# The first layer's mixtures and state layer, from three stages to one written order

## The chip, the cores and the metric

The kernel runs on one core of one Trainium2 chip, as one launch. The metric is the device time of that launch in microseconds, the median of several runs. A core has TensorE (PE, its weight loads PEld), VectorE (DVE), ScalarE (ACT), GpSimd (POOL), and SyncE (SP), whose queue issues most DMAs. Each engine works through a queue of its own and waits on semaphores for the other engines' results.

## What is computed

The input x has 4 sequences of 1024 tokens with 128 channels, all in 32-bit floats. Two layers follow; only the first one is touched here:

```
x = x + 0.5 * moe0(layernorm(x))
x = x + s6(layernorm(x))
x = x + 0.5 * moe0(layernorm(x))          # the same weights again
# the second layer: a capped mixture, attention over 16 wavelengths, the mixture again

moe0(h): probs = softmax(h @ w_router.T); w = the best two of 8, divided by their sum
         sum over those two of w_e * (relu(h @ w1_e.T)**2 @ w2_e.T)
         + relu(h @ ws1.T)**2 @ ws2.T     # shared, 256 hidden channels

s6(h):   u, res = split(h @ W_in)                      # 256 channels each
         u = silu(causal convolution of u over 3 tokens)
         dt, B, C = split(u @ W_x)                     # 8, 16, 16
         delta = softplus(dt @ W_dt + b_dt); A = -exp(A_log)
         s_n[t] = exp(delta * A_n) * s_n[t-1] + delta * u * B_n[t]     # n = 0..15
         y = sum over n of s_n * C_n + u * D
         return (y * silu(res)) @ W_out
```

## The kernel before, in words

x stays in SBUF as `x_sb`, tokens on partitions, 32 tiles of 128 tokens; a group is one sequence, 8 tiles. Three stages, `moe0`, `s6`, `moe0`, run one after another. In each, the tile framework's planner orders the instructions of every engine, from the order in the text, the dependencies and the number of buffers of each tile.

`moe0` computes every expert for every token and weighs with zero where a token did not choose it. For each group: `layernorm_t` (statistics on VectorE, normalized tiles transposed by TensorE, copied out by ScalarE), `route` (router logits, best two by rank counting), then for each half of 512 tokens two shared hidden units and eight experts. `hidden` is a matmul hp (L181), relu on ScalarE (L183), square on GpSimd (L185); hp has three PSUM buffers and h four, so several units are under way at once. The second matmul op (L195, L214) has three PSUM buffers, and VectorE adds each expert's result into x_sb with its weight, one tile of 128 tokens at a time (L218). A matmul of 32-bit floats is two passes on TensorE, so each appears twice in the counts.

`s6` works per sequence with channels on partitions (two halves c of 128). Input matmul pin (L264), convolution by three VectorE instructions (L273, L277), silu u (L285), W_x matmul into xd (L291, L298), then softplus by hand (L308 to L323: sp_v, sp_z, sp_w, delta, du). The recurrence runs in two stretches of 512 tokens. For each state n:

```
bp = sel[:, n].T @ xd        # TensorE spreads row n of B over 128 partitions (L334)
cp = sel[:, NS + n].T @ xd   # and row n of C (L336), copied to c_sb by ScalarE (L338)
for c in 0, 1:
    da = exp(delta * A_n)           # ScalarE (L341)
    db = du * bp                    # VectorE (L345)
    hst = scan(da, db)              # VectorE, the recurrence (L347)
    last = hst[:, 511]              # GpSimd, in the first stretch (L356)
    hm = hst * c_sb                 # GpSimd (L358)
    yp[c] += ident.T @ hm           # TensorE sums over n in PSUM (L359)
```

At its end y is formed (L364, L372), multiplied with W_out (L376) and added to x_sb (L384). The second mixture follows for all groups; then `moe1`, which uses `layernorm_t` and `route` too, the attention, whose TensorE and VectorE orders are written out by hand, and `moe1` again.

Of the kernel before, what the change touches and what calls it, by code (L numbers as in the profile page):

```python
# [20 lines left out]
I32 = mybir.dt.int32  # L21
# [55 lines left out]

def ln_stats(nc, sb, x, mv, rstd):

    n = x.shape[1]  # L80
    for i in range(n):
        st = sb.tile([P, nc.vector.BN_STATS_DIM], F32, name="ln_st", bufs=4)
        nc.vector.bn_stats(st, x[:, i, :])
        nc.vector.bn_aggr(mv[:, i, :], st)

    a = sb.tile([P, n], F32, name="ln_a")
    nc.vector.tensor_scalar(a, mv[:, :, 1], EPS, None, op0=ALU.add)
    q = sb.tile([P, n], F32, name="ln_q")
    nc.vector.tensor_scalar(
        rstd.bitcast(I32), a.bitcast(I32), -0.5, RSQRT, op0=ALU.mult, op1=ALU.add  # L90
    )
    for _ in range(3):
        nc.vector.scalar_tensor_tensor(q, rstd, -0.5, rstd, op0=ALU.mult, op1=ALU.mult)
        nc.vector.tensor_tensor(q, q, a, op=ALU.mult)
        nc.vector.scalar_tensor_tensor(rstd, q, 1.5, rstd, op0=ALU.add, op1=ALU.mult)
# [24 lines left out]
def route(nc, k, sb, ps, xnt, w_router, ex, mask):  # L120


    lg = ps.tile([P, GT, E], F32, name="lg", tag="tr")
    for i in range(GT):
        nc.tensor.matmul(lg[:, i, :], xnt[:, ts(i, P)], w_router, start=True, stop=True)
    mx = sb.tile([P, GT], F32, name="rt_mx")
    nc.vector.tensor_reduce(mx, lg, AX.X, ALU.max)
    d = sb.tile([P, GT, E], F32, name="rt_d")
    nc.vector.tensor_tensor(d, lg, mx[:, :, None].to_broadcast([P, GT, E]), op=ALU.subtract)
    nc.scalar.activation(ex, d, AF.Exp)  # L130
# [5 lines left out]
    eq = sb.tile([P, GT, E, E], F32, name="rt_eq")  # L136
    nc.vector.tensor_tensor(eq, other, own, op=ALU.is_equal)
    nc.vector.tensor_tensor(
        eq, eq, k.tri[:, None, :, :].to_broadcast([P, GT, E, E]), op=ALU.mult
    )  # L140
    above = sb.tile([P, GT, E, E], F32, name="rt_above")
# [6 lines left out]

def moe0(tc, k):


    nc = tc.nc
    with (
        tc.tile_pool(name="m0", bufs=2) as sb,
        tc.tile_pool(name="m0_tr", bufs=2, space=PSUM) as ps_tr,
        tc.tile_pool(name="m0_h", bufs=3, space=PSUM) as ps_h,
        tc.tile_pool(name="m0_o", bufs=3, space=PSUM) as ps_o,  # L160
    ):
        for g in range(B):
            xnt = sb.tile([P, L], F32, name="xnt")
            layernorm_t(nc, k, sb, ps_tr, g, xnt)
            ex = sb.tile([P, GT, E], F32, name="ex")
            mask = sb.tile([P, GT, E], F32, name="mask")
            route(nc, k, sb, ps_tr, xnt, k.wr0, ex, mask)

            w = sb.tile([P, GT, E], F32, name="w")
            nc.vector.tensor_tensor(w, ex, mask, op=ALU.mult)  # L170
            tot = sb.tile([P, GT], F32, name="tot")
            nc.vector.tensor_reduce(tot, w, AX.X, ALU.add)
            nc.vector.reciprocal(tot, tot)
            nc.vector.scalar_tensor_tensor(
                w, w, 0.5, tot[:, :, None].to_broadcast([P, GT, E]), op0=ALU.mult, op1=ALU.mult
            )

            def hidden(w1, cols):

                hp = ps_h.tile([P, 512], F32, name="hp")  # L180
                nc.tensor.matmul(hp, w1, xnt[:, cols], start=True, stop=True)  # L181
                r = sb.tile([P, 512], F32, name="r", bufs=3)
                nc.scalar.activation(r, hp, AF.Relu)  # L183
                h = sb.tile([P, 512], F32, name="h", bufs=4)
                nc.gpsimd.tensor_tensor(h, r, r, op=ALU.mult)  # L185
                return h

            for half in range(2):
                cols = ts(half, 512)
                t0 = g * GT + half * 4  # L190
                hs = [hidden(k.ws1[:, ts(f, P)], cols) for f in range(FS)]
                op = ps_o.tile([P, 4, C], F32, name="op")
                for i in range(4):
                    for f in range(FS):
                        nc.tensor.matmul(  # L195
                            op[:, i, :],
                            hs[f][:, ts(i, P)],
                            k.ws2[:, f, :],
                            start=(f == 0),
                            stop=(f == FS - 1),  # L200
                        )
                nc.vector.scalar_tensor_tensor(
                    k.x_sb[:, t0 : t0 + 4, :],
                    op,
                    0.5,
                    k.x_sb[:, t0 : t0 + 4, :],
                    op0=ALU.mult,
                    op1=ALU.add,
                )
                for e in range(E):  # L210
                    h = hidden(k.w1_0[:, e, :], cols)
                    op = ps_o.tile([P, 4, C], F32, name="op")
                    for i in range(4):
                        nc.tensor.matmul(  # L214
                            op[:, i, :], h[:, ts(i, P)], k.w2_0[:, e, :], start=True, stop=True
                        )
                    for i in range(4):
                        nc.vector.scalar_tensor_tensor(  # L218
                            k.x_sb[:, t0 + i, :],
                            op[:, i, :],  # L220
                            w[:, half * 4 + i, e : e + 1],
                            k.x_sb[:, t0 + i, :],
                            op0=ALU.mult,
                            op1=ALU.add,
                        )
# [5 lines left out]
def s6(tc, k):  # L231

    nc = tc.nc
    HL = 512
    with (
        tc.tile_pool(name="s6_c", bufs=1) as cst,
        tc.tile_pool(name="s6_b", bufs=2) as sb,
        tc.tile_pool(name="s6_w", bufs=3) as wk,
        tc.tile_pool(name="s6_tr", bufs=2, space=PSUM) as ps_tr,
        tc.tile_pool(name="s6_bc", bufs=2, space=PSUM) as ps_bc,  # L240
        tc.tile_pool(name="s6_y", bufs=1, space=PSUM) as ps_y,
    ):

        NR = DTR + 2 * NS
        sel = cst.tile([NR, 2 * NS, P], F32, name="sel")
        nc.vector.tensor_copy(sel, k.ident[0:NR, DTR:NR, None].to_broadcast([NR, 2 * NS, P]))
# [4 lines left out]
        for b in range(B):  # L251
            xnt = sb.tile([P, L], F32, name="xnt", bufs=1)
            layernorm_t(nc, k, sb, ps_tr, b, xnt)


            u = sb.tile([P, DI, L], F32, name="u")
            res = sb.tile([P, DI, L], F32, name="res")
            for c in range(2 * DI):
                if c < DI:
                    up = sb.tile([P, L + 2], F32, name="up", bufs=1)  # L260
                    nc.gpsimd.memset(up[:, 0:2], 0.0)
                for half in range(2):
                    pin = ps_tr.tile([P, HL], F32, name="pin", tag="tr")
                    nc.tensor.matmul(  # L264
                        pin, k.w_in[:, ts(c, P)], xnt[:, ts(half, HL)], start=True, stop=True
                    )
                    if c < DI:
                        nc.scalar.copy(up[:, 2 + half * HL : 2 + (half + 1) * HL], pin)
                    else:
                        nc.scalar.activation(res[:, c - DI, ts(half, HL)], pin, AF.Silu)  # L270
                if c < DI:
                    cv = sb.tile([P, L], F32, name="cv", bufs=1)
                    nc.vector.tensor_scalar(  # L273
                        cv, up[:, 0:L], k.w_conv[:, c, 0:1], None, op0=ALU.mult
                    )
                    for j in (1, 2):
                        nc.vector.scalar_tensor_tensor(  # L277
                            cv,
                            up[:, j : j + L],
                            k.w_conv[:, c, j : j + 1],  # L280
                            cv,
                            op0=ALU.mult,
                            op1=ALU.add,
                        )
                    nc.scalar.activation(u[:, c, :], cv, AF.Silu)  # L285

            xd = sb.tile([NR, L], F32, name="xd")
            for half in range(2):
                pxd = ps_tr.tile([NR, HL], F32, name="pxd", tag="tr")
                for c in range(DI):  # L290
                    nc.tensor.matmul(  # L291
                        pxd,
                        k.w_x[:, c, :],
                        u[:, c, ts(half, HL)],
                        start=(c == 0),
                        stop=(c == DI - 1),
                    )
                nc.scalar.copy(xd[:, ts(half, HL)], pxd)  # L298

# [862 lines left out]
```

## Time and profile before

| | us |
|---|---|
| median of 3 runs | 8650.8 |
| lowest and highest run | 8642.78, 8652.74 |
| the profiled execution's own time | 8645.76 |
| its span on the core | 8644.0 |
| first mixture stage, to about | 195 |
| state layer, about 195 to | 1111 |
| second mixture stage, last add at about | 1291 |

A window's row gives for each engine the time it was busy and the number of instructions, then the granted TensorE clock as a share of full speed. A group's row gives line, engine, operation, the tiles written and read, the count, the busy time in us with the mean ns of one, and the idle time of the engine just before them, with what ended it. In a waits row stand who waited, on whom, the total in us, the times and the longest. A busy TensorE is not TensorE at its peak: the end of a matmul is modelled, and its pipeline's latency is in it.

### The profile page before, as it was taken

The page shows a single profiled execution, that of the slowest core. Times are in us where ns is not written, and L with a number is a line of the kernel's source. Part 1 is how long each engine was busy: PE and PEld are TensorE (multiplying, and loading weights), DVE is VectorE, ACT ScalarE, POOL GpSimd, SP SyncE. Part 2 cuts the span into 40 slices and gives each one's busy share as a digit, 9 for nine tenths or more (in the row PEclk, how much of TensorE's full clock was granted, in tenths as well). Part 3 has the DMA queues.
Part 4 walks back from the last instruction along what each step waited for, and adds up shares of the span by engine and source line. Part 5 has one row for each costly group of instructions (what it writes and reads, how often), then busy time and mean ns, then how long its engine had stood idle before and what let it go on. Part 6 is the DMA issues. An engine that isn't in the chain of part 4 may idle for free. (4 is left out here: it accounts for less than half of the span.)

```text
span 8644.0 us, 174023 instructions
## 1 busy us (share of the span) xinstructions
PE 7278.9 (84%) x76602; PEld 3189.2 (37%) x76602; DVE 6580.4 (76%) x14818; ACT 7447.6 (86%) x1746; POOL 621.7 (7%) x642
## 2 busy tenths in 40 slices
PE   8888886888888888888888988888888888888885
PEld 5222253333333333333333433333334333333333
DVE  6766676777777777777777777777777777777773
ACT  2333324999999999999999999999999999999993
POOL 3554440000000000000000000000000000000000
PEclk9777797999999999999999999999999999999996
DMA  0000000000000000000000000000000000000000
GB/s 19 0 0 0 0 6 4 2 1 2 1 1 2 1 1 2 2 1 1 2 1 1 1 1 1 2 1 2 1 1 1 1 1 1 1 1 2 1 1 16
DMA packets 14660, 20.06 MB, mean 2 GB/s; under 512 B 3242, under 2 KB 12978, under 8 KB 13876
## 3 DMA queue, kind: packets, MB, share of 16 engines
q8 instruction: 611, 10.01, 0.5%
q1 hardware_dynamic: 9572, 6.01, 0.2%
q10 hardware_dynamic: 4304, 2.62, 0.1%
q14 instruction: 173, 1.42, 0.1%
HBM read 6.53 MB, written 2.10 MB: 1 GB/s over the span
## 5 line engine op out<-in xcount | busy, mean ns | idle before, releaser
L870 ACT ACTIVATE p_w<-xs,cc 128x7936 f32<-128x7936 f32 x1024 | 6971.4, 6898 | 92.3 <-PE o L880 73.9
L880 PE MATMUL o<-p_w,vt 128*9 128x256 f32 x63488 | 3829.5, 387 | 700.7 <-ACT p_w L870 695.2
L880 PEld LDWEIGHTS o<-p_w,vt 128*9 128x9 f32 x63488 | 1792.2, 92 | 2590.9 <-ACT p_w L870 1065.2
L789 DVE SCALAR_TENSOR_TENSOR x_p<-x_p,x_r 128x256 f32<-128x256 f32 x3072 | 1306.3, 425 | 105.4
L888 DVE COPY os<-o 128x256 f32<-128x256 f32 x1024 | 431.9, 422 | 580.4 <-PE o L880 579.5
L765 DVE COPY xs<-s 128x1024 f32<-128x1024 f32 x512 | 626.5, 1224 | 203.6 <-PE s L729 202.2
L743 DVE TENSOR_REDUCE nm<-s 128x1 f32<-128x1024 f32 x512 | 625.6, 1222 | 200.0 <-PE s L729 199.7
L880 PE MATMUL o<-p_w,vtop 128*9 128x256 f32 x2048 | 626.0, 388 | 9.8 <-DVE vtop L803 9.8
L906 PE MATMUL pt<-ident,os 128*128 128x128 f32 x2048 | 455.0, 304 | 168.7 <-DVE os L888 162.7
L729 PE MATMUL s<-kp,qp 32*128 32x512 f32 x2048 | 587.0, 650 | 0.7 <-DVE nm L743 0.7
L729 PE MATMUL s<-qp,kp 32*128 32x512 f32 x2048 | 583.1, 646 | 0.0
L906 PEld LDWEIGHTS pt<-ident,os 128*128 128x128 f32 x2048 | 208.2, 142 | 926.5 <-DVE os L888 789.0
L790 DVE SCALAR_TENSOR_TENSOR p_w<-x_p,x_e 128x256 f32<-128x256 f32 x1024 | 435.8, 426 | 109.4 <-DVE x_p L789 3.2
L359 PE MATMUL yp<-hm,ident 128*128 128x512 f32 x512 | 387.7, 878 | 105.5 <-POOL hm L358 103.9
L699 POOL COPY wp_q<-c_wq 128x32 f32<-128x32 f32 x32 | 6.9, 215 | 6151.4 <-PE pq L708 6151.4
L341 ACT ACTIVATE da<-delta,neg_a 128x512 f32<-128x512 f32 x256 | 182.7, 721 | 305.2 <-DVE hst L347 304.7
L787 DVE SCALAR_TENSOR_TENSOR x_p<-x_r 128x256 f32<-128x256 f32 x1024 | 429.1, 419 | 0.1
L781 DVE TENSOR_TENSOR x_r<-x_r,x_p 128x256 f32<-128x256 f32 x1024 | 428.5, 419 | 0.0
L358 POOL TENSOR_TENSOR hm<-hst,c_sb 128x512 f32<-128x512 f32 x256 | 369.9, 1457 | 172.6 <-ACT c_sb L338 119.7
L774 DVE TENSOR_SCALAR x_r<-xs,cc 128x256 f32<-128x256 f32 x1024 | 353.1, 345 | 1.0
L778 DVE TENSOR_SCALAR x_e<-x_p 128x256 int32<-128x256 f32 x1024 | 301.6, 295 | 35.0
L776 DVE TENSOR_SCALAR x_p<-x_r 128x256 f32<-128x256 f32 x1024 | 301.5, 294 | 35.0
(189 smaller groups left out, 4816.6 us busy)
## 6 DMA issues: line engine op xcount, KB each, us to landing
x_sb<-in_L_attn_x_dram ACTq DMA_DIRECT2D x4, 512.0 KB
c_w<-in_L_ffn_w_dram SPq DMA_DIRECT2D x4, 512.0 KB
out_dram<-x_sb SPq DMA_DIRECT2D x4, 512.0 KB
c_w<-in_L_ffn_w_stack_dram SPq DMA_DIRECT2D x1, 512.0 KB
c_w<-in_L_ffn_w_stack_dram ACTq DMA_DIRECT2D x1, 512.0 KB
c_ws<-in_L_ffn_ws_dram SPq DMA_DIRECT2D x2, 128.0 KB
c_w_in<-in_L_attn_W_in_dram SPq DMA_DIRECT2D x1, 256.0 KB
c_w_out<-in_L_attn_W_out_dram SPq DMA_DIRECT2D x1, 128.0 KB
```

Source lines behind the costliest of these rows:

```text
L359: nc.tensor.matmul(yp[c], k.ident, hm, start=(n == 0), stop=(n == NS - 1))
L729: nc.tensor.matmul(s[:, ts(half, 512)], a[row, ts(i, P)], c[row, ts(half, 512)], start=True, stop=True,)
L743: nc.vector.tensor_reduce(nm[:, i, 0:1], score(j, qp[n], i, kp[n]), AX.X, ALU.max, negate=True)
L765: nc.vector.tensor_copy(xs[u][:, i, :], score(j, kp[n], i, qp[n]))
L781: nc.vector.tensor_tensor(r, r, p, op=ALU.subtract)
L787: nc.vector.scalar_tensor_tensor(p, r, EXP2[4], r, op0=ALU.add, op1=ALU.mult)
L789: nc.vector.scalar_tensor_tensor(p, p, c, r, op0=ALU.add, op1=ALU.mult)
L790: nc.vector.scalar_tensor_tensor(p_w[g][:, 0, 0:SOFT], p, EXP2[0], e.bitcast(F32), op0=ALU.add, op1=ALU.mult,)
L870: nc.scalar.activation(p_w[g].rearrange("p a b -> p (a b)")[:, SOFT:], xs[u].rearrange("p a b -> p (a b)")[:, SOFT:], AF.Exp, scale=cc[:, ...
L880: nc.tensor.matmul(o[32 * r : 32 * r + D + 1, 0:QW], vtop[u] if soft else vts[b % 2][:, i, h, :], p_w[g][:, i, ts(r, QW)], start=(i == 0), ...
L888: nc.vector.tensor_copy(os, o[:, 0:QW])
L906: nc.tensor.transpose(pt[:, wl % 2 * 2 + c, :], os[:, ts(c, P)], k.ident)
```

## The change

`moe0` and `s6` become one stage, `layer0`. All five queues follow the order in which its text emits instructions. Its pieces are Python generators that yield after a small step, so that the steps of one can be laid between those of another.

- The mixtures are numbered m = 0 to 7: m < 4 is the first mixture of sequence m, m >= 4 the second of sequence m - 4. `route_rows` normalizes (by ScalarE's Identity with scale and shift), routes, and writes the square roots of the weights as 8 rows into DRAM; `weights` reads four of them back for a half, spread over 128 partitions by DMA. `experts` then scales relu(hp) by that root on GpSimd, squares on ScalarE, and sums all ten units of a half in one PSUM tile, which VectorE adds to x_sb once. hp and op have one PSUM buffer each.
- `prepare` folds the convolution into three accumulating matmuls with scaled copies w_cv of W_in, and writes the rows of B and C to DRAM. `states` takes 1024 tokens at once: rows of B and C arrive by DMA spread over 128 partitions (bc, three buffers, issued two states ahead), VectorE multiplies, scans, and a state later multiplies with C in place; the matmuls into y follow two states behind. `close` forms the output; its alternating partner is `softplus` of the next sequence.
- Beside the states of sequence b run the first mixture of b + 1 and, after it, the second of b - 1 and routing of others: three mixture steps for each of the first ten states, two afterwards. Mixture 0 and the second mixture of sequence 3 stand alone at the start and the end. After the first mixture of b + 1, one step of `prepare` is laid into each state.
- `route` is split (`best_two`, `rsqrt` become functions), with exp issued behind the ranking; `rt_eq` and `rt_above` have one buffer. `moe1` uses it too. w_conv is now loaded as rows spread over 128 partitions.

The core of the diff:

```diff
-def moe0(tc, k):
-def s6(tc, k):
...
+def layer0(tc, k):
+    HL = 512
...
+        tc.tile_pool(name="l0_y", bufs=1, space=PSUM) as ps_y,
+        tc.tile_pool(name="l0_t", bufs=1, space=PSUM) as ps_t,
+        tc.tile_pool(name="l0_r", bufs=1, space=PSUM) as ps_r,
+        tc.tile_pool(name="l0_h", bufs=1, space=PSUM) as ps_h,
+        tc.tile_pool(name="l0_o", bufs=1, space=PSUM) as ps_o,
+        tc.manual_schedule(engines=engines),
+    ):
         neg_a = cst.tile([P, DI, NS], F32, name="neg_a")
         nc.scalar.activation(neg_a, k.a_log, AF.Exp)
         nc.vector.tensor_scalar(neg_a, neg_a, -1.0, None, op0=ALU.mult)
+        w_cv = cst.tile([C, 3, DI * P], F32, name="w_cv")
+        for j in range(3):
+            nc.vector.tensor_tensor(w_cv[:, j, :], k.w_in[:, 0 : DI * P], ...)
...
+        def experts(m, half, after):
+            op = ps_o.tile([P, 4, C], F32, name="op")
+            for i in range(n + 2):                      # n = FS + E
+                if i == 1:
+                    weights(m, half, 1)
+                if i == 7 and after:
+                    weights(*after, 0)
+                if i >= 2:
+                    j = i - 2
...
+                    for a in range(4):
+                        nc.tensor.matmul(op[:, a, :], h[j][:, ts(a, P)], w2,
+                            start=(j == 0 and a == 0), stop=(j == n - 1 and a == 3))
+                if i < n:
...
+                    hp = ps_h.tile([P, HL], F32, name="hp")
+                    nc.tensor.matmul(hp, w1, m_x[m][:, ts(half, HL)], start=True, stop=True)
+                    r[i] = mb.tile([P, HL], F32, name="r", bufs=3)
+                    nc.scalar.activation(r[i], hp, AF.Relu, scale=ROOT if i < FS else 1.0)
+                if 1 <= i <= n:
+                    j = i - 1
+                    if j >= FS:
+                        e = j - FS
+                        nc.gpsimd.tensor_tensor(
+                            r[j], r[j], m_w[m, half, e // 4][:, e % 4, :], op=ALU.mult)
+                    h[j] = mb.tile([P, HL], F32, name="h", bufs=3)
+                    nc.scalar.activation(h[j], r[j], AF.Square)
+                yield
+            nc.vector.tensor_tensor(
+                k.x_sb[:, t0 : t0 + 4, :], k.x_sb[:, t0 : t0 + 4, :], op, op=ALU.add)
...
+        def states(b):
...
+            for s in range(NS + 2):
+                if s + 2 < NS:
+                    rows(s + 2)                         # DMA: B_n and C_n to 128 partitions
+                if s + 1 < NS:
+                    decay(s + 1)                        # ScalarE: two exp of 1024
+                if s < NS:
+                    for c in range(DI):
+                        hs[s, c] = sb.tile([P, L], F32, name="hs", bufs=6)
+                        nc.vector.tensor_tensor(hs[s, c], du[b][:, c, :], bc[s][:, 0, :], op=ALU.mult)
+                        nc.vector.tensor_tensor_scan(
+                            hs[s, c], da[s, c], hs[s, c], 0.0, op0=ALU.mult, op1=ALU.add)
+                if 1 <= s <= NS:
+                    for c in range(DI):
+                        t = hs[s - 1, c]
+                        nc.vector.tensor_tensor(t, t, bc[s - 1][:, 1, :], op=ALU.mult)
+                if s >= 2:
+                    for c in range(DI):
+                        for half in range(2):
+                            nc.tensor.matmul(y[b][c][half], k.ident, hs[s - 2, c][:, ts(half, HL)],
+                                start=(s == 2), stop=(s == NS + 1))
+                yield
...
+        run(route_rows(0))
+        weights(0, 0, 0)
+        run(route_rows(1), experts(0, 0, (0, 1)), experts(0, 1, (1, 0)))
+        run(prepare(0), softplus(0))
+        for b in range(B):
+            mix = beside(b)
...
+            for s, _ in enumerate(states(b)):
+                for _ in range(3 if s < 10 else 2):
+                    if next(mix, None) == "ready":
+                        ready = True
+                        ahead = prepare(b + 1)
+                if ready:
+                    next(ahead, None)
...
+            run(ahead)
+            for _ in both(close(b), softplus(b + 1) if b + 1 < B else ()):
+                next(mix, None)
+                next(mix, None)
+            run(mix)
+        run(route_rows(2 * B - 1))
+        weights(2 * B - 1, 0, 0)
+        run(experts(2 * B - 1, 0, (2 * B - 1, 1)), experts(2 * B - 1, 1, None))
...
-    (load0, (moe0, s6, moe0)),
+    (load0, (layer0,)),
```

`beside(b)` lays out, for b = 0: half 0 of mixture 1, route_rows(2), half 1 of mixture 1. For b = 1: the halves of mixture 2 around route_rows(4), then those of mixture 4 around route_rows(3). For b = 2: the halves of mixture 3 around route_rows(5), then those of mixture 5. For b = 3: route_rows(6), four empty steps, the halves of mixture 6. A half is 12 steps, a routing 6.

## The prediction

> **What bounds the kernel now.** I first cut the span into stages with the busy time by window, because the change touches only the first.
>
> ```profile
> 0.00:195.00 195.00, 166.94 (x896) 115.19 (x896) 129.58 (x502) 54.58 (x94) 83.81 (x96) 0.98 0.08 21
> 195.00:1111.00 916.00, 765.32 (x1312) 250.07 (x1312) 634.87 (x721) 344.53 (x496) 440.26 (x391) 0.76 0.00 0
> 1111.00:1291.00 180.00, 166.09 (x896) 114.67 (x896) 125.22 (x457) 53.16 (x92) 82.20 (x80) 0.96 0.00 1
> 1370.00:8644.00 7274.00, 6154.63 (x73390) 2687.30 (x73390) 5638.95 (x12889) 6986.32 (x1047) 13.30 (x62) 0.96 0.01 2
> ```
>
> Columns: stretch, its length, busy us of PE, PEld, DVE, ACT, POOL, then granted clock. Mixtures take 195 and 180, the state layer 916; all that can move is 1291 us. The rest, with ScalarE busy 6986 of 7274, stays. In the mixtures TensorE is the bound (167 of 195 at clock 0.98). In the state layer no engine is full and the clock is 0.76. The waits there and the groups:
>
> ```profile
> ACT da L341 <- DVE hst L347: 304.7, 172, 6.9
> DVE db L345 <- PE bp L334: 170.2, 93, 6.9
> ```
> ```profile
> L347 DVE TENSOR_TENSOR_SCAN hst<-da,db 128x512 f32<-128x512 f32 x128 | 167.1, 1342 | 5.6 <-POOL hm L358 4.4 <-ACT da L341 0.7
> L345 DVE TENSOR_TENSOR db<-du,bp 128x512 f32<-128x512 f32 x256 | 164.3, 682 | 171.0 <-PE bp L334 170.2
> L341 ACT ACTIVATE da<-delta,neg_a 128x512 f32<-128x512 f32 x256 | 182.7, 721 | 305.2 <-DVE hst L347 304.7
> L218 DVE SCALAR_TENSOR_TENSOR x_sb<-op,w,x_sb 128x128 f32<-128x128 f32 x512 | 137.7, 344 | 62.6 <-PE op L214 62.0
> L183 ACT ACTIVATE r<-hp 128x512 f32<-128x512 f32 x160 | 95.6, 597 | 207.7 <-PE hp L181 186.8 <-POOL h L185 20.9
> L323 DVE TENSOR_TENSOR du<-delta,u 128x1024 f32<-128x1024 f32 x8 | 9.8, 1224 | 0.3
> ```
>
> VectorE waits 170 us for the row matmul; the queues wait in turn on one another. Removing that wait is worth something only if no longer chain follows. The timeline of a mixture gives the links:
>
> ```profile
> 60.72 1.98 PE L181 MATMUL hp<-xnt,c_ws 128*128 128x512 f32 x4 [0.68 <-ACT xnt L117]
> 61.94 0.60 ACT L183 ACTIVATE r<-hp 128x512 f32<-128x512 f32 x1 [1.27 <-PE hp L181]
> 65.77 1.81 PE L195 MATMUL op<-c_ws,h 128*128 128x128 f32 x14
> ```
>
> From hp's start to relu's is 1.2 us; 14 op passes take 1.81, so an expert's eight take 1.0.
>
> **The change, part by part.**
>
> *States.* Gone: the sel matmuls (L334, L336: 512 passes), c_sb, last, hm on GpSimd. VectorE now does, per state and half of the channels, multiply, scan, multiply on 1024 columns. A 1024 multiply is 1.22 (du row). The scan's shortest 512 is 1.19; its extra 512 at two columns' time of a multiply gives 2.27. Per step 2 x (1.22 + 2.27 + 1.22) = 9.4 us; the old kernel needs 10.8 (173 per batch: scans of batch 1 run from 463 to 556 and 563 to 644). Port sharing: 46 of the 256 scans took some 1.05 us longer while GpSimd multiplied, about 0.12 per GpSimd operation; with three in a step 0.4, so 9.8. The Trainium skill (Advanced Engine Details and Errata, VectorE Performance Modes) says GpSimd and two-port VectorE instructions block each other; every operation blocking would give 3.2 instead of 0.4. I take the row; even 12.6 lies under the chain below. Decays (ScalarE, 0.72 for 512 columns, 1.15 for 1024, 2.3 a step) are hidden by TensorE's y matmuls. Where no mixture runs beside, TensorE holds only those (3.44 a step, 6.9 at half clock) and stays under VectorE.
>
> *Mixture step.* Each step queues on TensorE op(i-2), hp(i), on ScalarE relu(i), square(i-1). The next op needs that square, which stands behind relu(i), which needs hp(i), which stands behind op(i-2): one closed ring. op 1.0, hp to relu 1.2, relu and square 1.1 together, hand-over 0.06: 3.3 us at full clock, of which TensorE 1.86. The old loop ran hidden units ahead through three PSUM buffers at 1.9 us. GpSimd's multiply (1.27 with two sources, from hm's median) has 2 us of slack in the ring: nothing. L218's 138 us fall to 16 adds of 0.69, but VectorE did not bound there.
>
> *Clock.* TensorE's occupancy in the ring alone is 56%. The nearest row: the state loop, 16 passes of 512 columns at 0.43 us in ten, some 69%, was granted this:
>
> ```profile
> 300.00:350.00 50.00, 47.20 (x94) 16.78 (x93) 39.96 (x42) 18.18 (x29) 31.80 (x32) 0.85 0.00 0
> ```
>
> So I take 0.85 for woven steps and 0.75 for the ring alone. The Trainium skill (TensorE: Matmul & The Clock Gate, Part 1) makes the clock half or full and throttles after an idle window of about 3.4 us; the ring's gaps are 1.4 us, so by that rule the clock stays full. The trace falls to 0.85 with gaps under 2 us: I follow it. Ring alone: 1.44 + 1.86/0.75 = 3.9, a half mixture of eight full steps and four partial (8 us) 39; before, 195/8 = 24.4.
>
> *Woven step* (three mixture steps beside one state): at the joint TensorE puts four y matmuls (3.44) between hp and op. Work 3.44 + 3 x 1.86 = 9.0 over 0.85, plus two gaps of 1.44: 13.5 us, above VectorE's 9.8. A half takes four such steps, the first and last only part filled (10.7): 48.5.
>
> *Routing inside the states.* The add that ends a half waits for the last op and stands ahead of the next state in VectorE's queue, so VectorE enters with no lead and all is in a row: states 9.8, statistics and rsqrt (8 x 0.44 + 12 x 0.19) 5.8, then eight Identity on ScalarE through two buffers, with transposes, 5.4 (0.4 each, bounded by 0.25 of ex and 0.69 of sp_v), y and logits 5.5, best_two 4.6, weighting 2.9, rows out 3.5: 37.5 us for two states that cost 19.6.
>
> *Sum per batch.* Batch 0: halves 48.5 x 2, routing 37.5, six plain states with prepare's statistics 63, end 12: 210. Batches 1 and 2: 48.5 + 37.5 + 48.5, six states with two mixture steps and prepare (TensorE 3.44 + 3.72 + 2.6 = 9.8 over 0.9, plus 1.44: 12.3; earlier ones 11, statistics) 75, last two 24: 234 each. Batch 3: 37.5 + 10 + 97 + 47 + 8 = 199.
>
> *Between batches.* softplus is a chain over ScalarE and VectorE of 13 us per channel half, four table loads of 1.28 in it, two more from alternating with close: 32. With 15 mixture steps left (batch 1) 72, with 9 (batch 2) 54; close of batch 3 16.
>
> *Start.* neg_a and w_cv stand first in VectorE's queue and wait for a_log, issued at 9.6 us: statistics at 14 rather than 5.3 (w_conv, now 393 KB broadcast, is issued before a_log and covered by it; without that cover 1 to 2 us). Two routings in series: first hp at 60, against 16 now. Two halves 78. prepare and softplus of batch 0 62 (now some 42 from mixture to first scan; all softplus and tripled input matmuls, 32 x 0.86 more in all, come first). 200. *Tail:* routing 25, two halves 78: 103.
>
> *DMA and SP.* Per state 1 MB of rows, per half 2 MB of weights: 1.5 MB per 13.5 us, 110 GB/s. The first 50 us moved 78 GB/s at 0.29 busy, so about 270. SP waits for a free bc buffer with weights behind it; the weights have six mixture steps, some 20 us, to land. Nothing, if broadcast reads keep a third of that rate. moe1's exp waits only for d: nothing, at most 4 x 4 us were it held behind best_two.
>
> Together 200 + 210 + 32 + 234 + 72 + 234 + 54 + 199 + 16 + 103 = 1354 against 1291: +63. The profiled execution took 8645.8, 5 below the median of the runs: **8709 us**.
>
> **The rivals.**
> 1. *The clock stays full* in ring and woven steps. Ring 3.3, half woven 44, and with it preludes and tail: about 98 less, 1256: 8611. For it: dense mixtures got 0.98, and a woven step is fuller than the state loop. Against: the row above. It decides once the woven clock passes about 0.93. Chance 0.20.
> 2. *VectorE sets the pace*, the ring being shorter than I read it. VectorE's sum is 604 + 106 + 23 + 56 + 29 + 11 = 829; its share inside the states, 688, plus start 200, between-batch chains 120 and tail 103 make 1110: 8465. For it: VectorE loses its 170 us wait and 138 us of L218. Against: the ring is queue order, not load. Chance 0.18.
> 3. *Rows arrive late.* If 128 reads of one row give under 110 GB/s, each of 64 states stretches; at 60 GB/s to 25 us, +740. Square shows in no row: were it in another table than Exp, two loads of 1.28 around most mixture steps add up to 490. Chance 0.06.
> 4. *The gains and chains cancel*: the clock lands between, 8634 to 8668. Chance 0.10.
>
> **How the numbers follow.** A measurement here can tell 0.2%, 17 us. My chain has 0.46. Faster is rivals 1 and 2, 0.38; same 0.10; slower 0.52. The likeliest case alone spans 8670 to 8790 (clock 0.92 to 0.75, VectorE blocked by each GpSimd multiply). The range reaches down to half of rival 2 and up beyond the chain's worst: 8490 to 8800, leaving out about 0.09 on each side.
>
> **What would show it.** Right: in the woven stretch a relu waits on hp and an op on the square, VectorE idle a quarter; hp to hp 3.3 to 4 us; clock near 0.85; first hp at 60 us; last mixture alone 78 us. Wrong: VectorE over 90% busy there, clock 1.0, or VectorE's hs waiting on the row DMA.

## The result, and the profile after

The changed kernel takes 8632.4 us (median of 14 runs, 8625.68 to 8636.08), the kernel before 8646.6 in the same comparison (14 runs, 8638.17 to 8654.76). The ratio is 0.9982, with a 95% interval of 0.9973 to 0.9990: faster by some 14 us, 0.18%. The prediction was 8709, slower. The time lies inside its range, but its sign and the mechanism behind the sign were wrong.

The stretches of the profile after (columns as before: stretch, length, busy us of PE, PEld, DVE, ACT, POOL, granted clock, DMA share, GB/s):

```profile
0.00:197.00 197.00, 93.54 (x314) 46.98 (x314) 45.67 (x149) 60.99 (x101) 21.59 (x33) 0.91 0.23 71
197.00:1190.00 993.00, 667.00 (x2174) 341.25 (x2174) 808.45 (x811) 391.55 (x550) 181.78 (x96) 0.83 0.26 89
1190.00:1289.00 99.00, 55.01 (x240) 32.78 (x240) 23.97 (x151) 30.87 (x56) 20.29 (x16) 0.83 0.15 43
1370.00:8625.00 7255.00, 6128.71 (x73356) 2668.08 (x73354) 5633.07 (x12871) 6985.71 (x1047) 13.00 (x60) 0.96 0.01 2
```

The first layer now ends at 1288.5 instead of 1291: two separate mixture stages became 197 and 99 us, and what lay in them went into the middle stretch, which grew from 916 to 993. VectorE is busy 81% of that stretch, against 69% before. The last row (ScalarE 6986 of 7255) is the second layer, attention above all, as before.

The groups of the new loop between 195 and 1190, and then the waits:

```profile
L442 DVE TENSOR_TENSOR_SCAN hs<-da,hs 128x1024 f32<-128x1024 f32 x128 | 316.1, 2470 | 12.6
L439 DVE TENSOR_TENSOR hs<-du,bc 128x1024 f32<-128x1024 f32 x128 | 182.6, 1427 | 0.0
L448 DVE TENSOR_TENSOR hs<-hs,bc 128x1024 f32<-128x1024 f32 x128 | 177.4, 1429 | 0.0
L324 POOL TENSOR_TENSOR r<-r,m_w 128x512 f32<-128x512 f32 x96 | 181.8, 1894 | 803.4 <-issue 536.3 <-ACT r L317 265.8 <-POOL r L324 1.2
```
```profile
ACT r L317 <- PE hp L315: 239.9, 106, 4.6
PE op L305 <- ACT h L328: 117.4, 85, 8.5
ACT da L424 <- DVE hs L442: 112.8, 32, 10.8
DVE u L485 <- ACT res L476: 100.9, 16, 12.8
```

The ring is there (relu on hp, op on the square), but VectorE's three groups show next to no idle time ahead of them. VectorE's wait on the row matmul is gone, and ScalarE's wait ahead of the decays fell from 304.7 to 112.8 us. The only large wait of VectorE is in `close` (L485 on the silu of the gate). No wait of VectorE on a DMA appears. The durations matter: the multiply was costed at 1.22 and measures 1.43, the scan 2.27 and measures 2.47.

A woven half, a mixture alone, and states with no mixture beside them:

```profile
279.00:320.00 41.00, 31.52 (x126) 17.17 (x125) 40.28 (x23) 18.22 (x28) 17.21 (x8) 1.00 0.40 138
81.00:142.00 61.00, 34.99 (x177) 21.07 (x176) 4.39 (x19) 19.70 (x35) 19.01 (x15) 1.00 0.17 52
323.00:398.00 75.00, 51.74 (x106) 19.68 (x104) 60.22 (x68) 22.52 (x30) 0.00 (x0) 0.88 0.17 60
```

In the first row TensorE has its full clock and VectorE is busy 40.28 of 41 us. In the second the ring alone has the full clock too, with TensorE busy 57%. These two stretches were taken where the clock was full. It is lower where the states run alone (0.88), in the chains of `prepare`, softplus and routing (0.69 from 142 to 196 us, 0.56 from 1190 to 1220), and at the start of a half: the first mixture steps beside sequence 0 ran at half clock until 217.5 us, 5.0 us each. The ring, link by link, in the timeline:

```profile
82.38 1.16 PE L305 MATMUL op<-c_w,h 128*128 128x128 f32 x8 [1.26 <-ACT h L328]
83.37 1.02 PE L315 MATMUL hp<-m_x,c_w 128*128 128x512 f32 x2
84.49 0.60 ACT L317 ACTIVATE r<-hp 128x512 f32<-128x512 f32 x1 [2.17 <-PE hp L315]
84.98 0.62 ACT L328 ACTIVATE h<-r 128x512 f32<-128x512 f32 x1
85.66 1.16 PE L305 MATMUL op<-c_w,h 128*128 128x128 f32 x8 [1.26 <-ACT h L328]
```

From op to op 3.28 us: the ring as it was drawn in the prediction, at its full-clock price.

### The profile page after: what moved, and what is told of

It reads as the page before. It is cut to its first block, busy times and chain, and to the rows that moved or that the text cites. A ratio compares the mean times of both kernels' runs of the same rounds, so it can differ in the third digit from the quotient of the medians.

```text
span 8625.6 us, 171896 instructions
## 1 busy us (share of the span) xinstructions
PE 6981.5 (81%) x76218; PEld 3116.2 (36%) x76218; DVE 6557.7 (76%) x14152; ACT 7476.8 (87%) x1767; POOL 239.2 (3%) x220
## 5 line engine op out<-in xcount | busy, mean ns | idle before, releaser
L317 ACT ACTIVATE r<-hp 128x512 f32<-128x512 f32 x160 | 95.3, 596 | 328.2 <-PE hp L315 328.0
L442 DVE TENSOR_TENSOR_SCAN hs<-da,hs 128x1024 f32<-128x1024 f32 x128 | 316.1, 2470 | 12.6
L452 PE MATMUL y<-hs,ident 128*128 128x512 f32 x512 | 270.8, 678 | 35.6 <-DVE hs L448 35.6
L942 PE MATMUL pt<-ident,nm 128*64 128x128 f32 x1024 | 188.2, 361 | 98.6 <-DVE nm L938 98.6
```

## The experiments

A woven state is one that has mixture steps laid beside it. Two theories stood against each other. *Ring*: the woven steps (12.2 us) follow the closed ring of hp, relu, square and op, now at full clock. *Port*: they follow VectorE, whose instructions with two SBUF operands stop while GpSimd multiplies. Four kernels make a square of the two.

**swap: hp and relu issued ahead of op.** The ring is opened; the work is the same.

```diff
+                if i < n:
+                    hp = ps_h.tile(...); nc.tensor.matmul(hp, w1, ...)
+                    nc.scalar.activation(r[i], hp, AF.Relu, ...)
                 if i >= 2:
                     for a in range(4): nc.tensor.matmul(op[:, a, :], ...)
-                if i < n:
-                    hp = ps_h.tile(...); nc.tensor.matmul(hp, w1, ...)
-                    nc.scalar.activation(r[i], hp, AF.Relu, ...)
```

> Edit: in every mixture step the hidden matmul hp and its relu are issued ahead of the second matmul op, so the ring op - hp - relu - square is cut and a mixture step can shrink from 3.3 us to TensorE's own 1.9. Ring theory (the ring paces the woven steps): the four halves that run alone fall from 33 to about 21 us (48 in all), the woven steps of three from 12.2 to VectorE's own 9.8 (some 22 of them, 53), between the batches some 15 less: about 8515. Port theory (VectorE, blocked by each GpSimd multiply, paces the woven steps): those stay at 12.2, only the halves alone and the stretches between the batches gain: about 8570.

8558.7 us (ratio 0.9896, 0.9881 to 0.9912). The ring alone falls from 3.3 to 1.8 us a step, a half mixture alone from 33 to 21 us, and the last add of the layer comes at 1219.1 instead of 1287.8. But the woven states are no shorter: the first four take 7.0, 13.4, 12.5 and 10.3, together 43.2, where the changed kernel has 7.0, 10.3, 12.2 and 12.2, together 41.7. The time lies between the two expected ones, nearer to Port's 8570. GpSimd and VectorE side by side in its timeline:

```profile
177.39 1.20 DVE L439 TENSOR_TENSOR hs<-du,bc 128x1024 f32<-128x1024 f32 x1
177.77 1.94 POOL L324 TENSOR_TENSOR r<-r,m_w 128x512 f32<-128x512 f32 x1 [70.03 <-issue]
178.69 3.18 DVE L442 TENSOR_TENSOR_SCAN hs<-da,hs 128x1024 f32<-128x1024 f32 x1
181.13 6.22 POOL L324 TENSOR_TENSOR r<-r,m_w 128x512 f32<-128x512 f32 x3 [1.42 <-ACT r L306]
181.79 4.44 DVE L448 TENSOR_TENSOR hs<-hs,bc 128x1024 f32<-128x1024 f32 x2
186.15 2.29 DVE L439 TENSOR_TENSOR hs<-du,bc 128x1024 f32<-128x1024 f32 x1
188.53 2.29 DVE L442 TENSOR_TENSOR_SCAN hs<-da,hs 128x1024 f32<-128x1024 f32 x1
```

While GpSimd's three multiplies run (181.1 to 187.4), three VectorE multiplies take 6.7 us instead of 3 x 1.2. The scan after them takes 2.29, the one that begins beside the first GpSimd multiply 3.18. GpSimd pays as well: 6.22 for three, where the ring alone has 1.27 each.

**nomul and swapnomul: GpSimd's multiply taken out**, from the changed kernel and from swap.

```diff
-                        nc.gpsimd.tensor_tensor(
-                            r[j], r[j], m_w[m, half, e // 4][:, e % 4, :], op=ALU.mult
-                        )
```

> Edit: GpSimd's multiply of relu with the root of the weight is left out, so every expert counts with weight one; nothing else changes. Ring theory: the ring still takes 11.8 us per woven step: about 8620, VectorE's instruction times as they were. Port theory: VectorE's 1024-column multiplies fall from a mean of 1.43 to 1.22 us and the scan from 2.47 to 2.27, the steps with two mixture steps fall from 10.3-11.3 to 9.3 (12 of them, 16 us), the steps with three only to the ring's 11.8: about 8605.

> Both edits: hp and relu ahead of op, and GpSimd's multiply by the weights left out. Ring theory: as with the swap alone, about 8515, at most 10 less. Port theory: woven steps fall to 9.4 us, 2.6 to 2.8 less in some 22 steps and 1 to 2 in twelve, 75 below the swap alone: about 8495.

8835.5 us (1.0216, 1.0202 to 1.0230) and 8728.8 (1.0096, 1.0080 to 1.0111). Without the weights the second layer receives other values and computes experts that it passes over otherwise, so the totals say nothing; the first layer is compared by the time of its last relu:

| last relu of the layer, us | GpSimd multiplies | none |
|---|---|---|
| ring closed (as changed) | 1284.5 | 1239.9 |
| ring open (swap) | 1215.7 | 1129.4 |

Opening the ring is worth 69 us, taking the multiply out 45, both 155. Neither alone gets the whole, because the other then binds: with the ring closed, three woven states take 9.3, 9.4 and 11.8; with both gone, all with three mixture steps take 9.3, VectorE's own sum. In nomul, with the ring closed, VectorE's multiplies and scans are at 1.21 and 2.29 us, as Port had it. VectorE's durations in swap, then in swapnomul (its lines are two lower):

```profile
L442 DVE TENSOR_TENSOR_SCAN hs<-da,hs 128x1024 f32<-128x1024 f32 x122 | 288.5, 2365 | 12.0
L448 DVE TENSOR_TENSOR hs<-hs,bc 128x1024 f32<-128x1024 f32 x126 | 196.1, 1598 | 0.0
L439 DVE TENSOR_TENSOR hs<-du,bc 128x1024 f32<-128x1024 f32 x122 | 167.7, 1375 | 0.0
```
```profile
L440 DVE TENSOR_TENSOR_SCAN hs<-da,hs 128x1024 f32<-128x1024 f32 x122 | 279.6, 2292 | 12.0
L437 DVE TENSOR_TENSOR hs<-du,bc 128x1024 f32<-128x1024 f32 x121 | 146.3, 1209 | 0.0
L446 DVE TENSOR_TENSOR hs<-hs,bc 128x1024 f32<-128x1024 f32 x124 | 144.5, 1210 | 0.0
```

The differences, 0.073, 0.388 and 0.166 us, over 128 of each are 80 us; the last relu moved by 86. The same sum for the changed kernel (2470, 1429, 1427 against the lower rows) is 0.18 + 0.22 + 0.22 over 128, or 79 us.

**cpool: the multiply with C on GpSimd**, where the old kernel had it.

```diff
-                        nc.vector.tensor_tensor(t, t, bc[s - 1][:, 1, :], op=ALU.mult)
+                        nc.gpsimd.tensor_tensor(t, t, bc[s - 1][:, 1, :], op=ALU.mult)
```

> Edit: the multiply of the states with C goes from VectorE to GpSimd, the change without its fourth part. Ring theory: VectorE falls to 7.0 us per state and paces nothing, the 24 plain states fall from 9.3 to about 7: about 8575. Port theory: GpSimd's two multiplies of 1024 columns (2.5 us each, from 1.27 for 512) and VectorE's two-input instructions exclude each other: a plain state takes 7.0 + 5.0 = 12.0 instead of 9.3, a woven one up to 15.8 instead of 12.2: about 8780.

8708.5 us (1.0071, 1.0056 to 1.0086). A quarter of VectorE's work leaves it, and the layer gets 73 us longer (last relu 1357.3):

```profile
L442 DVE TENSOR_TENSOR_SCAN hs<-da,hs 128x1024 f32<-128x1024 f32 x119 | 413.2, 3473 | 12.1 <-DVE hs L439 0.5
L448 POOL TENSOR_TENSOR hs<-hs,bc 128x1024 f32<-128x1024 f32 x116 | 368.6, 3192 | 318.3 <-DVE hs L442 243.3 <-issue 64.4 <-PE pw L276 10.5
```

The scan goes from 2.47 to 3.47 us. Port has the sign, at about half the expected size; ring has the wrong sign. So the part of the change that gives VectorE this multiply does pay.

**fine: swap, with the weight in VectorE's read of hp, and mixture steps between VectorE's instructions.** GpSimd is empty; VectorE reads hp from PSUM.

```diff
-                        nc.gpsimd.tensor_tensor(r[j], r[j], m_w..., op=ALU.mult)
+                        nc.vector.scalar_tensor_tensor(
+                            r[i], hp, 0.0, m_w..., op0=ALU.max, op1=ALU.mult)
```

> Edit on top of the swap: the weight multiply goes from GpSimd into VectorE's read of hp in PSUM (max with 0, times the weight row, one instruction for relu and multiply), and the three mixture steps of a state are laid between VectorE's instructions of that state instead of behind them. Port theory: an instruction that reads PSUM is not blocked and GpSimd is silent, so a woven step is 9.3 + 3 x 0.69 = 11.4 instead of 12.5, one with two mixture steps 10.7 instead of 11.4, multiplies at 1.21 and scans at 2.29: about 8525. Rival (queue order): hp now waits for VectorE's queue, whose scans take 2.3 us, the ring comes back through it and woven steps reach 13: about 8580.

8575.0 us (0.9917, 0.9904 to 0.9931): 16 above swap, near the higher of the two expected times. VectorE's scans are back at 2.29 us, but it carries the new reads:

```profile
L442 DVE TENSOR_TENSOR_SCAN hs<-da,hs 128x1024 f32<-128x1024 f32 x124 | 284.2, 2292 | 9.5 <-ACT da L424 0.5
L310 DVE SCALAR_TENSOR_TENSOR r<-hp,m_w 128x512 f32<-128x512 f32 x92 | 62.3, 677 | 60.6 <-PE hp L304 59.3 <-ACT h L328 1.3
```

128 reads of 0.68 are 87 us, just what the blocking cost (80 to 86), so VectorE gains nothing. The halves that stand alone still take 21 us (a step 1.98 instead of 1.81). The woven ones of sequence 0 are longer, 44.7 and 47.5 us instead of swap's 43.2 and 45.2, with states of up to 13.1, as the rival had it. The two edits were not tried apart.

**swapspread: swap, with the routing's steps laid one behind every third mixture step** instead of in a row.

```diff
-            yield from experts(b + 1, 0, (b + 1, 1))
-            yield from route_rows(then)
-            yield from experts(b + 1, 1, (then, 0))
+            yield from spread(route_rows(then),
+                experts(b + 1, 0, (b + 1, 1)), experts(b + 1, 1, (then, 0)))
```

> Edit on top of the swap: the six steps of a routing are laid one after every third mixture step instead of in a block, so that none of them waits for the one before. Queue theory (the block costs what its waits cost, 35 us for two states): each of four or five routings gives back some 12 us: about 8500. VectorE theory (the engine is full: ten states with two halves and a routing are 93 + 16 x 1.05 + 13 = 123 us, and 124 are measured): nothing is to be had: about 8555.

8547.7 us (0.9887, 0.9872 to 0.9903), 11 under swap. The runs of the two do not overlap (8544.5 to 8554.4, 8556.0 to 8561.8), the intervals of their ratios do. The two states of sequence 0 that held a whole routing took 15.5 and 20.2; spread, only one takes over 15.5 (17.9). VectorE is busy 173.75 of the 179 us from 173 to 352. Little slack was left in the queue order, as the VectorE theory (8555) had it.

**before_rows128: the old kernel with its row matmuls over 128 partitions instead of 40**, zeros below. This asks where the clock of 0.85 came from that the prediction had taken.

```diff
-        sel = cst.tile([NR, 2 * NS, P], F32, name="sel")
+        sel = cst.tile([P, 2 * NS, P], F32, name="sel")
-            xd = sb.tile([NR, L], F32, name="xd")
+            xd = sb.tile([P, L], F32, name="xd")
+            nc.vector.memset(xd, 0.0)
```

> The kernel before, with the row matmuls of B and C over all 128 partitions (xd and sel filled with zeros below row 40) instead of 40; same passes, same columns. Height theory (the clock follows how much of the array a pass uses): the state layer's granted clock rises from 0.76 to above 0.9, the passes shorten and the kernel takes some 40 us less, about 8605. Idle theory (the clock follows the gaps alone): clock and time stay, 8645 to 8655.

8647.1 us (1.0002, 0.9994 to 1.0011). Three windows of the state loop, in the kernel before and then in this one:

```profile
323.00:422.00 99.00, 89.39 (x168) 30.11 (x168) 81.97 (x81) 33.56 (x51) 55.95 (x42) 0.86 0.00 0
463.00:556.00 93.00, 73.53 (x109) 22.62 (x110) 65.58 (x68) 33.92 (x50) 59.03 (x60) 0.70 0.00 0
563.00:644.00 81.00, 76.57 (x134) 24.80 (x132) 63.32 (x62) 28.98 (x44) 44.03 (x30) 0.79 0.00 1
```
```profile
323.00:422.00 99.00, 76.57 (x167) 27.16 (x165) 87.70 (x82) 35.94 (x55) 60.30 (x46) 1.00 0.00 0
463.00:556.00 93.00, 61.84 (x96) 21.57 (x96) 59.76 (x63) 33.88 (x48) 54.60 (x53) 0.72 0.00 0
563.00:644.00 81.00, 64.78 (x145) 23.38 (x144) 74.55 (x69) 31.48 (x48) 47.70 (x34) 1.00 0.00 1
```

In the first window as many matmuls with as many columns, and the clock rises from 0.86 to 1.00 although TensorE is busy 13 us less; so its lower clock belonged to the matmuls over few partitions. This window and the third lie mostly in the second 512 tokens of a sequence. In the first 512 tokens (second window) the clock hardly rises, 0.70 to 0.72. There TensorE is busy 66% of the time, in the other two 77 and 80%; between 500 and 552 us the clock changes between full and half though no wait of TensorE is over 2.2 us. Over the whole state layer it goes from 0.76 to 0.86, short of the expected 0.9.

The unchanged time is a sum of two changes. From first scan to last, the second 512 tokens of sequence 1 take 75.9 us instead of 82.7, the first 512 take 101.9 instead of 94.2, with the same instructions in the same order; the other sequences are alike. So the full clock did shorten the loop where it came. Why the first 512 tokens became longer is open.

**before_route: the old kernel with only the new route().**

```diff
+def best_two(nc, sb, lg, d, mask, tri): ...
-    nc.scalar.activation(ex, d, AF.Exp)        # ahead of the ranking
+    best_two(nc, sb, lg, d, mask, k.tri)
+    nc.scalar.activation(ex, d, AF.Exp)        # behind it
```

> The kernel before, with only route() of the change (best_two, exp behind the ranking, one buffer for rt_eq and rt_above). If the second layer's mixture starts earlier because of the new routing: about 8636. If it does so because VectorE stands idle beside the last mixture and runs its statistics there: 8648, no change.

8646.0 us (0.9995, 0.9987 to 1.0003). The new routing function is not where the 14 us come from.

**after_late: the changed kernel, with one VectorE instruction that holds the second layer's statistics behind the last add.**

```diff
         run(experts(2 * B - 1, 0, ...), experts(2 * B - 1, 1, None))
+        nc.vector.tensor_scalar(k.x_sb[:, :, 0:1], k.x_sb[:, :, 0:1], 1.0, None, op0=ALU.mult)
```

> The changed kernel with one VectorE instruction more: it multiplies one column of all 32 token tiles by 1 in place, behind the last add of the first layer, so that the second layer's statistics can only start after it. If some 11 us of the gain come from those statistics running beside the last mixture, the first ranks of the second layer come about 15 us after the last add instead of 9, and the time goes from 8632.4 to 8638 to 8644. If they come from elsewhere (the second layer's routing, the attention), it stays within 2 us of 8632.4.

8647.5 us (0.9998, 0.9989 to 1.0006): the gain is gone (the interval just touches that of the changed kernel). It is 15 us above the changed kernel, more than the 6 to 12 expected. VectorE's timeline at the end of the layer, changed kernel first, then this one:

```profile
1254.96 0.69 DVE L330 TENSOR_TENSOR x_sb<-x_sb,op 128x512 f32<-128x512 f32 x1 [39.22 <-PE op L305]
1255.69 0.87 DVE L96 BATCH_NORM_STATS2 ln_st<-x_sb 128x6 f32<-128x128 f32 x4
1287.83 0.69 DVE L330 TENSOR_TENSOR x_sb<-x_sb,op 128x512 f32<-128x512 f32 x1 [31.27 <-PE op L305]
...
1297.19 0.69 DVE L145 TENSOR_REDUCE rt_rank<-rt_above 128x64 f32<-128x512 f32 x1
```
```profile
1289.89 0.20 DVE L577 TENSOR_SCALAR x_sb<-x_sb 128x32 f32<-128x32 f32 x1
1290.13 0.49 DVE L96 BATCH_NORM_STATS2 ln_st<-x_sb 128x6 f32<-128x128 f32 x2
...
1304.86 0.68 DVE L145 TENSOR_REDUCE rt_rank<-rt_above 128x64 f32<-128x512 f32 x1
```

In the changed kernel VectorE has nothing to do beside the last mixture (39 and 31 us idle ahead of its two adds), so the second layer's statistics of what is finished run there: 24 of the 32 between 1192 and 1204 us, beside the routing, and four more between the adds. Held back, they start at 1290.1 and the first ranking comes at 1304.9, about where the kernel before has it (1305.9). The rankings after it follow suit: attention's first work on its phases (cs_k) comes at 1341.2 us in the changed kernel, at 1354.1 in this one and at 1355.0 in the kernel before, so nearly the whole 14 us are there by then.

**early: swapspread, with the first half of mixture 1 laid into `prepare` and softplus of sequence 0, and that of mixture 2 into the end of sequence 0.**

```diff
-        run(prepare(0), softplus(0))
+        early = {m: experts(m, 0, (m, 1)) for m in range(1, B)}
+        for piece in (prepare(0), softplus(0)):
+            for _ in piece:
+                next(early[1], None)
+                next(early[1], None)
```

> On top of the version with hp ahead and the routing spread (8547.7 us): the first half of batch 1's mixture is laid into the preparation and softplus of batch 0 (115 to 173 us, TensorE 28.9 of 58 us busy, GpSimd idle), and what mixture steps of batch 2 fit go into the end of batch 0. Port theory: every GpSimd multiply that leaves the states returns about 0.67 us to VectorE (86 us over 128), and a woven state falls from 12.5 to 9.3; 16 multiplies and some eight woven states, 10 to 25 us, against some 3 to 6 us that ScalarE and TensorE add to the two softplus chains: 8525 to 8540. Rival: those chains are bound by ScalarE's and TensorE's order, each mixture step of 1.8 us goes onto them whole, 24 steps are 43 us, and nothing is left: 8550 to 8570.

8536.8 us (0.9873, 0.9858 to 0.9888), the fastest of all (its runs lie at 8532.8 to 8539.8, those of swapspread at 8544.5 to 8554.4; the intervals of the two ratios overlap). The time is inside Port's 8525 to 8540, but not all by Port's way. The last add of the layer comes at 1195.7 instead of 1207.8. In sequence 0 the move only breaks even: the first scan starts 9 us later (at 181.7 instead of 172.7), the sixteen states take 170 us instead of 179. The 12 us come from sequence 1, which takes 255 us from its first state to the next sequence's instead of 271: its states are some 6 us longer, but the stretch between them and the next first state falls from 79 to 59 us, with fewer mixture steps left over for it (4 GpSimd multiplies instead of 11). This run also lays the routing beside sequences 0 and 1 more densely, one step behind every mixture step, and the two edits were not tried apart.

## Why the prediction was wrong

**The step that failed is the clock of the woven steps and of the ring.** "So I take 0.85 for woven steps and 0.75 for the ring alone … The trace falls to 0.85 with gaps under 2 us: I follow it." Once under way, both ran at 1.00; only the first steps after a pause ran at 0.50. The Trainium skill's rule (TensorE: Matmul & The Clock Gate, Part 1: half or full, throttled after an idle window), which the prediction had weighed and set aside, was right for the ring: gaps of 1.3 us, clock 1.00. It does not cover the old loop, where before_rows128 fell to half clock between 500 and 552 us with no wait over 2.2 us. The nearest row was not near enough: half of the matmuls in that loop ran over 40 partitions, the woven steps have none of those, and before_rows128 shows the second 512 tokens of the same loop at 1.00 without them. What the sum becomes, term by term:

| term | predicted | measured |
|---|---|---|
| ring alone, a step | 3.9 | 3.3 |
| half mixture alone | 39 | 33 (37 to 39 where it starts at half clock) |
| woven state | 13.5 | 12.2 |
| half mixture woven | 48.5 | 41.6 to 44.1 (the first: 7.0 + 10.3 + 12.2 + 12.2) |
| two states with a routing | 37.5 | 35.8 |
| start to the first state | 200 | 196 |
| sequence 0, to the next first state | 242 | 236 |
| sequence 1 | 306 | 289 |
| sequence 2 | 288 | 272 |
| sequence 3 | 215 | 199 |
| tail | 103 | 98 |
| layer | 1354 | 1288.5 |

Of the 65 us, some 38 are the eight woven halves (six at 43 in the mean instead of 48.5, the two of sequence 3 together 91 instead of 97), 14 the four halves that stand alone (142 instead of 156), and 13 the routings in the states. The rest cancels. The layout of the sum (what is in a row, what lies beside what) held; what paces a woven state did not, as follows. Of the signs named in advance, two that were to show it wrong came: VectorE over 90% busy in the woven stretch, and clock 1.00.

**A second term was mis-sized and hidden under the first: blocking at the shared port.** The prediction took 0.4 us a step from 46 long scans of the old trace, and named 12.6 us a state as what the Trainium skill's rule (Advanced Engine Details and Errata, VectorE Performance Modes) would make of it: GpSimd and two-port VectorE instructions block each other. In swap, where the ring no longer binds, three woven states take 13.4, 12.5 and 10.3, in the mean 12.1: the trace agrees with the page. The old trace misled because two of its three large VectorE groups did not show it: L345, which reads PSUM, takes 656 to 690 ns in all 256 cases, and L218, which does too, 334 to 352; only the scans could. The multiplies that the change moves to SBUF operands show it most. In the changed kernel the ring's price (two gaps of 1.44 and 9.0 of TensorE, 11.9 at full clock) and VectorE's (12.2 as measured) lie so near each other that neither alone frees the step, as the square shows.

**The rivals.** Rival 1, the full clock, had that step right and gave 8611, 21 too low. Its ring (3.3) and its woven half (44) are what was measured; they make 60 of its 98 us. Most of the other 38, in what comes before and between, did not come: there the clock was still low (0.69 and 0.56 in the windows named above). Rival 2, VectorE as the bound at 8465, was half right: VectorE was full in the woven steps (40.28 of 41), but with longer instructions than its sum had, and ring, chains and routings kept the rest. With ring and blocking both gone (swapnomul) the last relu came at 1129 us, near its 1110 for the layer. Rival 3 did not occur: the rows came at 89 GB/s in the mean and 138 in woven steps, with no wait of VectorE on them, and no table load stands at Square (L328). Rival 4, that gains and chains cancel, fits the layer's 2.5 us but not by its reason: the clock of the woven steps did not land between.

**What the sum did not hold** is the 14 us themselves. It ended at the layer's last add, on "The rest … stays". The layer's own gain is 2.5 us in the profiled runs, and after_late, which keeps it, is 1.5 us from the kernel before, which cannot be told from nothing. The measured gain is the second layer's statistics, moved beside the last mixture; after_late, which takes only that away, returns the whole of it. That they could move because VectorE no longer adds every expert there (L218, 512 instructions of 344 ns) is likely, but no run shows it. So the sign of the measured change came from outside the sum; the layer itself ended within 2.5 us of where it had ended before.

## What to carry to other kernels

Before a clock is carried from one loop to another, compare the shape of the matmuls and not only TensorE's fill; a rule and a row that disagree call for the difference between the two loops, not for the nearer number. Work given to GpSimd is not free where VectorE is full with SBUF operands: price each such instruction as VectorE time (here 0.6 to 0.7 us for 512 columns), and look for a place where VectorE idles (in early's sequence 0 that only broke even) or reads PSUM. A sum over one stage should also ask what the next stage can start earlier when an engine falls idle at the end.

## What was not expected of the hardware

- Matmuls over 40 of 128 partitions went with a granted clock of 0.86 (323 to 422 us) where the same loop over 128 had 1.00, with equal counts and columns; where TensorE was busy only 66% of the time (463 to 556 us), the clock stayed low either way (0.70, 0.72). The added rows hold zeros; from which number of partitions on the clock stays full was not tried.
- Blocking is mutual: a GpSimd multiply of 512 columns took 1.27 us alone, 1.89 beside the states, 2.14 in swap. With 1024 columns on GpSimd beside them (cpool) it took 3.19, and VectorE's scan 3.47 instead of 2.29.
- With the fuller matmuls half of the old state loop became faster (82.7 to 75.9 us) and the other half slower (94.2 to 101.9), so that the total did not move (1.0002). A total that stays is no sign that nothing changed.
